# Row transposes by transposing transfers, two VectorE additions by accumulating transfers, and a new instruction order, in a four-layer graph-attention kernel

## Chip, cores and metric

The kernel runs on one core of a Trainium2 chip. The metric is the device time of one execution in microseconds. Three runs of the kernel before took 2677.28, 2681.27 and 2683.81 us, a median of 2681.27 us.

## What is computed

Eight graphs (batches) share one adjacency matrix of 2048 nodes; every node has 128 features. Four layers follow each other. Each normalises the rows of x, clips them at zero, attends over the neighbours and adds the result to x:

```python
h = jnp.maximum(_layernorm(x), 0.0)
# layers 0, 1, 3: scores are an outer sum
Wh = h @ W                       # layer 0: h @ W.T; layer 3: h = h*(node_weights+1) + node_bias before
                                 # W, and then a layer norm with ln_gamma, ln_beta on Wh
e = leaky_relu((Wh @ a1)[:, :, None] + (Wh @ a2)[:, None, :], 0.2)
p = softmax(where(adj > 0, e, -9e15))
out = p @ Wh                     # layer 0: elu(out); layer 1: out; layer 3: elu(out + Wh)
# layer 2: 4 heads of 32 features, scores from products
p = softmax(where(adj == 0, -inf, leaky_relu(h_head @ h_head.T, 0.2)))
out = p @ h_head
x = x + out
```

## The kernel before

**Units.** A unit is one layer of one batch, 32 in all: class Gat for layers 0, 1 and 3, class Heads for layer 2. A unit begins with row statistics (moments: BN_STATS on VectorE, a power on GpSimd). `rows_made` then makes the normalised rows h in four quarters of 512 rows on ScalarE (L538, for layer 3 also L545). `transposes` (L569) turns a quarter with four 128x128 TensorE transposes into PSUM, because the following products contract over features. In Gat, ScalarE copies the turned quarter to SBUF (`h_t`, L590), TensorE multiplies it with W and the two score vectors (L599), and ScalarE writes the weighted rows y and the exponential factors of the scores (L637 to L652). In Heads, the turned quarter is written as a coarse part `hi` (ScalarE, L964) and a rest `lo` (VectorE, L968); both go out to DRAM (L973), as do the rows themselves (`values`, L952), and come back by head as `s`, `m` and `v` (L987, L995, L1000).

**Tokens.** Gat's attention for half of the target nodes (1024) and one block of 128 source nodes is a token, 768 in all. VectorE makes the masked weights in one operation (`zg`, L767, named front), and TensorE multiplies them with y in eight products (L776, named back).

**Beats.** In Heads one head and one block of 128 source nodes is a beat, 512 in all: scores on TensorE in two pieces (L1063), two exponentials on ScalarE (L1070), one mask multiplication on VectorE (L1076), and sums by 32-column products on TensorE (`weigh`, L1085). These are issued for two beats at a time, for batch 7 for one.

**Ends.** `out` divides the sums of a half by their denominators (L808, L809). For layers 0 and 3 it then forms elu as two parts: an exponential (`oe`) and a clipped copy (`oa`), both at L815. VectorE adds min(exp, 1) to x (`elu_e`, L839), and the clipped part is added to x by an accumulating transfer that GpSimd issues (`plus_a`, L845). The -1 of elu is in x from the start: -2 is added to it once for both elu layers. Layer 3 also needs rows3's part (a transfer, L893), a multiplication by gamma (L832) and an addition of beta (L834) on VectorE. A head ends in `finish`: a division (L1105) and an accumulating transfer into x (L1110), issued by GpSimd.

**Order.** Nothing is scheduled by hand at the instructions. Every instruction group is registered with `add(engine, us, due, emit, needs, takes, frees, lag)`: an assumed duration, a due time, what it needs, which buffers it takes and frees, and a lag until its result is visible to others. `Plan.run` plays this list through and fixes the order on each of the five queues (TensorE, VectorE, ScalarE, GpSimd, and SP, which issues most transfers). All queues run in that order. Due times come from the tables TOKENS, BEATS and LEADS. Two PSUM slots named `pair` serve scores, transposes, projections and other short products.

Of the kernel before, what the change touches and what calls it, by code (L numbers as in the profile page):

```python
# [8 lines left out]
F32 = mybir.dt.float32  # L9
F32R = mybir.dt.float32r  # L10
BF16 = mybir.dt.bfloat16
I32 = mybir.dt.int32
U8 = mybir.dt.uint8
F8 = mybir.dt.float8e4
# [26 lines left out]
def adj_preln_d4(ctx: ExitStack, tc: tile.TileContext, x, adj, w0, a0, w1, a1, w3, a3,  # L41
# [112 lines left out]
    class Op:  # L154
# [6 lines left out]
    HURRY_US, WINDOW_US, BEAT_SUMS_US = 54.8, 0.148, 0.86  # L161

    EARLY = dict(front=30.31, score=69.21, exp=-934.15, mask=-178.47, sums=-6.09)

    SINGLY, GROUP = (7,), 2
# [3 lines left out]
    PLUS_US, PLUS_LAG_US, GATHER_US, GATHER_LAG_US = 1.0, 5.5, 2.2, 6.5  # L169


    SHIFTS = {
        30: 0.0, 93: 0.0, 113: 0.0, 115: 0.0, 121: 0.0, 131: 0.0, 135: 0.0, 139: 0.0, 143: 0.0, 147: 0.0,
        151: 0.0, 1041: 0.0, 1099: 0.0, 2060: 0.0, 2063: 0.0, 2886: 0.0, 2890: 0.0, 3168: 0.0, 3549: 0.0,
        5962: 0.0, 6178: 0.0, 6183: 0.0,
    }

    class Plan:
# [3 lines left out]
        LAG = dict(PE=0.3, ACT=0.22, DVE=0.15, POOL=0.2, SP=2.5)  # L182
        SAME = True
        ENTER_US, LEAVE_US = 0.09, 0.21
# [6 lines left out]
        def add(self, engine, us, due, emit, needs=(), takes=(), frees=(), lag=None, tiled=False):  # L191
            due += SHIFTS.get(len(self.ops), 0.0)
            op = Op(engine, us, due, emit, needs, takes, frees, self.LAG[engine] if lag is None else lag, tiled)
            self.ops.append(op)
            return op
# [56 lines left out]
    def fast(ctx):  # L252
# [9 lines left out]
        plan = Plan(dict(pair=(4, 6), sums=(0,), more=(1,), low=0, z=5, zg=3, r=2, h=3, h_t=2, hi=1, lo=1,  # L262
# [184 lines left out]
        class Unit:  # L447
# [15 lines left out]
            def moments(self, name, part, rows, needs):  # L463
# [21 lines left out]
                for q in range(4):  # L485
                    last = [add("DVE", 0.72, self.due(part + 0.03 * q), lambda op, q=q: stats(op, q),
                                last + list(needs[q]), takes=["st"] + ["norm"] * (name == "x") if q == 0 else [])]
                    if q == 0:
                        self.normal = taker = last[0]
                begun = add("DVE", 0.5, self.due(part + 0.11), begin, last, takes=["var"], frees=[("st", taker)])  # L490
                last = [add("POOL", 3.4, self.due(part + 0.12), power, [begun])]
# [37 lines left out]
            def rows_made(self, part, step):  # L529
# [4 lines left out]
                def rows(op, q):  # L534
                    self.h[q] = blocks(quarter("h", bufs=3))
# [27 lines left out]

            def transposes(self, q, part, made, takes):
# [6 lines left out]
                return add("PE", 0.45, self.due(part), turn, made[1:], takes=["pair"] + takes,  # L571
                           frees=[("h", made[0])])

        class Gat(Unit):
            def beginning(self):
# [6 lines left out]
                for q in range(4):  # L582
                    part = 0.2 + step * q
                    turn = self.transposes(q, part, made[q], ["h_t"])
# [3 lines left out]
                    def copy(op, q=q, turn=turn, begins=begins):  # L588
# [3 lines left out]
                    copied = add("DVE" if begins else "ACT", 0.61 if begins else 0.47, self.due(part), copy,  # L592
                                 [turn], frees=[("pair", turn)])
# [8 lines left out]
                    product = add("PE", 0.9, self.due(part + 0.03), project, [copied, projected[layer]],  # L602
# [10 lines left out]
                    ends.append(add("ACT", 0.55 if layer == 3 else 1.25, self.due(part + 0.05),  # L613
# [40 lines left out]
            def second(self, ends):  # L654
# [15 lines left out]
                scored = add("DVE", 0.7, self.due(0.8), scores, [last])  # L670
                powers = add("ACT", 0.3, self.due(0.81), exps, [scored])
                factored = add("DVE", 0.3, self.due(0.82), factors, [powers])
# [11 lines left out]
            def spread(self):  # L684
# [33 lines left out]
                if ROWS_TURNED:  # L718
# [14 lines left out]
                    turned = add("PE", 0.12, at, turn_rows, last, takes=["pair"])  # L733
                    last = add("ACT", 0.25, at, copy_rows, [turned], frees=[("pair", turned)])
                    self.written = add("SP", 0.5, at, write_rows, [last], lag=2.5)
# [4 lines left out]
            def targets(self, half, due):  # L740
# [9 lines left out]
                op = add("SP", 0.5, due, read, [self.written], takes=["r"], lag=6.5)  # L750
# [9 lines left out]
            def token(self, a, due, place, last_front, last_back, first, last, gate=None):  # L760
# [11 lines left out]
                def back(op):  # L772
                    z = self.z.pop(a)
                    for i in range(HB):
# [10 lines left out]
                b = add("PE", 1.785, due, back, [f, last_back, self.v_ready[jb // 4]],  # L785
                        takes=[name] + ["pair"] * place if first else [], frees=[("zg", f)])
# [9 lines left out]
            def out(self, half, back, place, name, due):  # L796
# [15 lines left out]
                def whole(op, into, func):  # L812
                    if into == "e" and "e" not in key:
                        key["e"] = big.tile([P, HB, C], F32, tag="oe", name="oe", bufs=1)
                    nc.scalar.activation(key[into], key["a"], func)  # L815

# [47 lines left out]
                else:  # L864
                    last = taker = add("DVE", 1.75, due - 30, divided, [back], takes=["oa"])
# [15 lines left out]
                if layer == 0:  # L881
                    e = e_taker = add("ACT", 0.95, due + 6, lambda op: whole(op, "e", AF.Exp), [last], takes=["oe"])
                    last = add("ACT", 0.95, due + 8, lambda op: whole(op, "a", AF.Relu), [e])
                else:
# [10 lines left out]
                    for k in range(L3_DMA and b != B - 1, 3):  # L895
                        last = add("DVE", 1.14, due + 6 + 4 * k, lambda op, k=k: wide3(op, k), [last] + rows)
                    e = add("ACT", 0.95, due + 18, lambda op: whole(op, "e", AF.Exp), [last])
# [24 lines left out]
                e = add("DVE", 1.14, late, elu_e, [e], frees=[("oe", e_taker)])  # L922
# [13 lines left out]
                last = add("SP", 0.5, late + 6, write, [last])  # L936
# [3 lines left out]
        class Heads(Unit):  # L940
            def beginning(self):
# [13 lines left out]
                for q in range(4):  # L955
                    part = 0.25 + step * q
                    kept = add("SP", 0.5, self.due(part), lambda op, q=q: keep(op, q), [kept, made[q][1]],
                               lag=2.5)
                    self.there.append(kept)
                    turn = self.transposes(q, part, made[q], ["hi", "lo"])  # L960

                    def high(op, q=q, turn=turn):
                        self.h_t[q, 0] = quarter("hi", F32R, 1)
                        nc.scalar.copy(self.h_t[q, 0], ps[:, turn.got["pair"], :])  # L964

                    def low(op, q=q, turn=turn):
                        self.h_t[q, 1] = quarter("lo", F32R, 1)
                        nc.vector.tensor_sub(self.h_t[q, 1], ps[:, turn.got["pair"], :],  # L968
                                             self.h_t[q, 0].bitcast(F32))
# [6 lines left out]
                    hi = add("ACT", 0.47, self.due(part), high, [turn])  # L976
                    lo = add("DVE", 0.61, self.due(part), low, [hi], frees=[("pair", turn)])
                    for k, (tag, op) in enumerate((("hi", hi), ("lo", lo))):
                        self.there.append(add("SP", 1.9, self.due(part + 0.02), lambda op, q=q, k=k: store(op, q, k),
                                              [op, kept], frees=[(tag, turn)], lag=2.5))  # L980

            def load(self, h, due):
# [29 lines left out]
                s0 = add("SP", 2.1, due, lambda op: source(op, 0), there, takes=["s"], lag=3.0)  # L1012
                m = add("SP", 1.0, due, target, there, takes=m_taken, lag=7.5)
                self.first_target = [m]
                m_taker = m if m_taken else held
                s1 = add("SP", 2.1, due + 4, lambda op: source(op, 1), self.there, takes=["s"], lag=3.0)
                v = add("SP", 0.5, due, values, self.there, takes=["v"], lag=5.5)
                return s0, s1, m, v, m_taker

            def beats(self, heads):  # L1020
# [4 lines left out]
                for h, (start, step) in enumerate(heads):  # L1025
                    ops = self.load(h, start - 24.0)
                    for jb in range(NB):
# [3 lines left out]
                        for c2 in range(2):  # L1031
                            score = add("PE", 0.463, due - EARLY["score"] + c2, lambda op, s=s, c2=c2: self.scores(op, s, c2),
                                        [score, ops[jb // HB], ops[2]], takes=["pair"] + ["z"] * (c2 == 0))
                            if c2 == 0:
                                z_taker = score
                            exps.append(add("ACT", 1.0, due - EARLY["exp"] + c2, lambda op, s=s, c2=c2, sc=score: self.exp(
# [380 lines left out]
```

## Time and profile before

| what | value |
|---|---|
| median of three runs | 2681.27 us |
| the profiled execution | 2679.22 us |
| its span, first to last instruction | 2677.4 us |
| granted TensorE clock, mean | 0.992 |

The largest groups of work, from the page's list of costliest groups:

| engine, line, what | count | busy us | mean ns |
|---|---|---|---|
| TensorE L776, products of tokens | 12288 | 1472.5 | 276 |
| TensorE L1063, scores of beats | 2048 | 627.0 | 421 |
| TensorE L1085, sums of beats | 4096 | 499.7 | 601 |
| TensorE L569, transposes of rows | 512 | 79.7 | 280 |
| VectorE L1076, masks of beats | 512 | 1160.0 | 2285 |
| VectorE L767, fronts of tokens | 768 | 969.4 | 1279 |
| ScalarE L538, rows | 512 | 207.0 | 485 |
| GpSimd L113, powers | 31 | 122.1 | 3940 |

Matmuls overlap in the pipeline, so a group's mean is the latency of one instruction; the pace is read from the starts of neighbouring groups in the timeline. A product of 4-byte values appears as two instructions. The waits say what a queue stood still for; the longest of TensorE's own (columns: us in total, times, longest) are 10.9 us for ScalarE's exponentials and 10.0 us for VectorE's fronts.

### The profile page before, as it was taken

Reading aid. Unit: us, or ns where it says so; the run is one execution under the profiler, and the core shown is the slowest. Engines: PE = TensorE matmul, PEld = TensorE weight load, DVE = VectorE, ACT = ScalarE, POOL = GpSimd, SP = SyncE. Lnnn points to the kernel's source line nnn. Section 1 sums busy time; section 2 is a strip of 40 time slices with the busy share of each in tenths; the row PEclk is TensorE's granted clock in tenths of the full one; section 3 lists DMA queues with packets and bytes.
Section 4 is the critical chain, followed back from the end, with each engine's and each line's share of the span. In section 5 each row is a group of like instructions: output and inputs, shape, how many; then the busy total and the mean of one; then the engine's idle time right before and its main releaser. Section 6 shows DMA issues by size and latency. Waiting matters only on the chain. (4 is left out here: it accounts for less than half of the span.)

```text
span 2677.4 us, 49161 instructions
## 1 busy us (share of the span) xinstructions
PE 2598.6 (97%) x20104; PEld 2041.9 (76%) x20104; DVE 2482.8 (93%) x3304; ACT 1719.8 (64%) x2777; POOL 279.8 (10%) x143
## 2 busy tenths in 40 slices
PE   7999999999999999999999999999999799999997
PEld 7899877687777786888777768787766478676587
DVE  8867989989999999999999999999999799999987
ACT  2526555767776677647766778674676866778751
POOL 1200000010100110011110101011101110010020
PEclk9999999999999999999999999999999999999999
DMA  9002423144344332362424434424315321542121
GB/s 319 17 9 63 97 52 67 10 94 103 81 88 99 62 62 56 60 123 56 86 50 87 79 78 87 82 48 88 72 42 93 64 40 56 115 68 64 33 52 34
DMA packets 216875, 196.49 MB, mean 73 GB/s; under 512 B 142896, under 2 KB 178176, under 8 KB 210496
## 3 DMA queue, kind: packets, MB, share of 16 engines
q1 hardware_dynamic: 144112, 156.46, 22.5%
q0 software_dynamic: 72112, 36.73, 12.0%
q8 instruction: 160, 2.62, 0.4%
q14 instruction: 75, 0.61, 0.1%
q10 hardware_dynamic: 416, 0.07, 0.0%
HBM read 123.03 MB, written 33.73 MB: 59 GB/s over the span
## 5 line engine op out<-in xcount | busy, mean ns | idle before, releaser
L776 PEld LDWEIGHTS ps<-y,zg 128*128 128x128 f32 x12288 | 1449.5, 192 | 66.1 <-DVE zg L767 17.0
L776 PE MATMUL ps<-y,zg 128*128 128x129 f32 x12288 | 1472.5, 276 | 13.6 <-DVE zg L767 10.0
L1070 ACT ACTIVATE z<-ps,shift 128x1024 f32<-128x1024 f32 x1024 | 1091.1, 1111 | 525.4 <-PE ps L1063 513.4
L1076 DVE SCALAR_TENSOR_TENSOR z<-z,edge 128x2048 f32<-128x2048 f32 x512 | 1160.0, 2285 | 26.9 <-ACT z L1070 26.6
L767 DVE SCALAR_TENSOR_TENSOR zg<-r,cr,edge 128x1024 f32<-128x1024 f32 x768 | 969.4, 1279 | 113.6 <-PE ps L776 101.9
L1063 PE MATMUL ps<-m,s 128*128 128x512 f32 x2048 | 627.0, 421 | 21.8 <-ACT z L1070 10.9
L1063 PEld LDWEIGHTS ps<-m,s 128*128 128x128 f32 x2048 | 341.0, 190 | 268.4 <-ACT z L1070 147.8
L1085 PE MATMUL ps<-z,v 128*32 128x512 f32 x4096 | 499.7, 601 | 1.5 <-DVE z L1076 1.3
L1085 PEld LDWEIGHTS ps<-z,v 128*32 128x32 f32 x4096 | 103.9, 109 | 223.8 <-issue 175.0
L538 ACT ACTIVATE h<-x,nmrx,rstdx 128x128 f32<-128x128 f32 x512 | 207.0, 485 | 48.5 <-DVE nmrx L118 36.0
L113 POOL TENSOR_TENSOR rstdx<-varx,neg_half 128x16 f32<-128x16 f32 x31 | 122.1, 3940 | 458.0 <-DVE varx L108 444.6
L1110 POOL DMA_DIRECT2D x<-o x31 | 65.8, 2124 | 747.9 <-DVE o L1105 608.2
L845 POOL DMA_DIRECT2D x<-oa x40 | 36.9, 922 | 748.5 <-ACT z L1070 199.5
L599 PE MATMUL ps<-rhs,h_t 128*128 128x130 f32 x768 | 104.9, 283 | 4.6 <-DVE h_t L590 2.7
L599 PEld LDWEIGHTS ps<-rhs,h_t 128*128 128x128 f32 x768 | 95.4, 195 | 12.6 <-ACT h_t L590 7.1
L471 DVE BATCH_NORM_STATS2 st<-x 128x6 f32<-128x128 f32 x496 | 100.4, 278 | 3.3 <-DMA x<-oa 3.3
L569 PE MATMUL ps<-ident,h 128*128 128x128 f32 x512 | 79.7, 280 | 4.2 <-ACT z L1070 1.7
L809 DVE TENSOR_TENSOR oa<-ps,rs 128x384 f32<-128x384 f32 x144 | 73.9, 513 | 5.1
L815 ACT ACTIVATE oe<-oa 128x1024 f32<-128x1024 f32 x32 | 33.9, 1058 | 69.0 <-DVE oa L834 55.3
L590 ACT COPY h_t<-ps 128x512 f32<-128x512 f32 x92 | 52.6, 585 | 33.2 <-PE ps L569 33.1
L569 PEld LDWEIGHTS ps<-ident,h 128*128 128x128 f32 x512 | 60.9, 143 | 16.6 <-ACT h L538 4.3
L637 ACT ACTIVATE y<-ps,y 128x128 f32<-128x128 f32 x240 | 68.6, 369 | 0.0
(129 smaller groups left out, 833.8 us busy)
## 6 DMA issues: line engine op xcount, KB each, us to landing
s<-halves SPq DMA_DIRECT2D x256, 128.0 KB, 2.8
m<-halves SPq DMA_DIRECT2D x64, 512.0 KB, 6.8
r<-row SPq DMA_DIRECT2D x42, 512.0 KB, 3.9
x<-oa POOLq DMA_DIRECT2D x40, 512.0 KB, 4.9
raw<-in_adj_dram SPq DMA_DIRECT2D x16, 1024.0 KB, 15.5
values<-h SPq DMA_DIRECT2D x32, 256.0 KB, 2.3
halves<-hi SPq DMA_DIRECT2D x128, 64.0 KB, 1.7
halves<-lo SPq DMA_DIRECT2D x128, 64.0 KB, 1.7
```

What stands on the lines that cost most here:

```text
L113: nc.gpsimd.tensor_tensor(out=rstd, in0=v, in1=neg_half, op=OP.pow)
L471: nc.vector.bn_stats(out=key["st"][:, n, :], in_=rows()[:, n, :])
L538: nc.scalar.activation(self.h[q][:, k, :], X[self.b][:, n, :], AF.Relu, scale=key["rstd"][:, n:n + 1], bias=key["nmr"][:, n:n + 1])
L569: nc.tensor.transpose(pk[:, k, :], self.h[q][:, k, :], ident)
L599: nc.tensor.matmul(pv[:, k, :C + 2], lhsT=self.h_t[q][:, k * P:(k + 1) * P], rhs=rhs, start=True, stop=True)
L767: nc.vector.scalar_tensor_tensor(z, self.r[half], self.cr[:, 0, jb:jb + 1], edge[:, jb, half * HN:(half + 1) * HN], op0=OP.max, op1=OP.mult)
L776: nc.tensor.matmul(ps[:, self.banks(half, place)[i // 3], k * CE:(k + 1) * CE], lhsT=z[:, i * P:(i + 1) * P], rhs=self.y[:, jb, :], start= ...
L809: nc.vector.tensor_mul(key["a"][:, i0:i1, :], pv[:, :, :C], r[:, i0:i1, None].to_broadcast([P, i1 - i0, C]))
L1063: nc.tensor.matmul(ps[:, lo + c, :], lhsT=self.S[h, jb // HB][:, at:at + P], rhs=self.M[h][:, (c2 * 2 + c) * 512:(c2 * 2 + c + 1) * 512], ...
L1070: nc.scalar.activation(self.z[s][:, c2 * HN:(c2 + 1) * HN], ps[:, lo:lo + 2, :].rearrange("p b t -> p (b t)"), AF.Exp, bias=shift)
L1076: nc.vector.scalar_tensor_tensor(self.z[s], self.z[s], 1.0, edge[:, jb, :], op0=OP.mult, op1=OP.mult, accum_out=self.den[:, h, jb:jb + 1])
L1085: nc.tensor.matmul(ps[c * HD:(c + 1) * HD, 0, :], lhsT=self.V[h][:, jb, :], rhs=z[:, c * 512:(c + 1) * 512], start=jb == 0, stop=jb == NB - 1,
```

## The change

1. The transposes of 25 of the 32 units leave TensorE; `ON_PE` lists the seven that stay. A quarter h is split on ScalarE into two planes of 16-bit halves (`pl`), one transposing transfer issued by SP turns both planes (`tr`), and ScalarE merges them to `h_t`. In Heads, `hi` and `lo` are then made from `h_t` in SBUF instead of PSUM; `lo` is written over `h_t`.
2. elu's exponential becomes exp(min(a, 0)), made by two ScalarE passes (`below`: clip of -a; `grown`: exponential of its negative) in place of one. Being at most 1, it needs no minimum, and an accumulating transfer issued by GpSimd adds it to x; batch 7 and the units in DIRECT keep VectorE.
3. Layer 3's addition of beta becomes an accumulating transfer too, except for batch 7.
4. The planner's assumed durations, lags and constants are other ones. TOKENS becomes a sequence of halves at equal steps (HALVES), in another order; BEATS becomes a list of 33 places between which a head's 16 beats are spread evenly; LEADS has other values. The empty SHIFTS go.
5. Buffers: h has two in place of three, `lo` goes, `pl` and `tr` have one each.

```diff
-    SINGLY, GROUP = (7,), 2
+    PLANES, TURNED, ON_PE = 1, 1, ((0, 0), (1, 0), (0, 1), (0, 2), (7, 1), (7, 2), (7, 3))
+    SPLIT_US, MOVE_US, MOVE_LAG_US, MERGE_US = 0.94, 1.28, 5.2, 1.207
+    GROUPS = (2, 2, 2, 2, 2, 2, 2, 2, 2, 2, 2, 2, 2, 2, 2, 2, 2, 2, 2, 2, 2, 2, 2, 2, 2, 2, 2, 2, 1, 1, 1, 1)
...
-        LAG = dict(PE=0.3, ACT=0.22, DVE=0.15, POOL=0.2, SP=2.5)
+        LAG = dict(PE=0.2, ACT=0.14, DVE=0.135, POOL=0.2, SP=1.6)
...
+            def turned_by_transfer(self, q, part, made, kept=None):
+                key = {}
+                def split(op):
+                    key["pl"] = big.tile([P, 2, 4 * P], U16, tag="pl", name="pl", bufs=PLANES)
+                    nc.scalar.copy(key["pl"], self.h[q].rearrange("p k c -> p (k c)").bitcast(U16).rearrange(
+                        "p (n two) -> p two n", two=2))
+                def move(op):
+                    key["tr"] = big.tile([P, 8, P], U16, tag="tr", name="tr", bufs=TURNED)
+                    nc.sync.dma_start_transpose(out=key["tr"], in_=key["pl"].rearrange("p two n -> p (two n)"))
+                def merge(op):
+                    self.h_t[q] = quarter("h_t")
+                    nc.scalar.copy(self.h_t[q].bitcast(U16).rearrange("p (n two) -> p two n", two=2),
+                                   key["tr"].rearrange("p (two k) n -> p two (k n)", two=2))
+                parted = add("ACT", SPLIT_US, self.due(part), split, made[1:], takes=["pl"], frees=[] if kept else [("h", made[0])])
+                moved = add("SP", MOVE_US, self.due(part), move, [parted, kept], takes=["tr"],
+                            frees=[("pl", parted)] + [("h", made[0])] * (kept is not None),
+                            lag=MOVE_LAG_US)
+                return add("ACT", MERGE_US, self.due(part), merge, [moved], takes=["h_t"], frees=[("tr", moved)])
...
+                def below(op):
+                    key["e"] = key.get("e") or big.tile([P, HB, C], F32, tag="oe", name="oe", bufs=1)
+                    nc.scalar.activation(key["e"], key["a"], AF.Relu, scale=-1.0)
+                def grown(op):
+                    nc.scalar.activation(key["e"], key["e"], AF.Exp, scale=-1.0)
...
-                    e = e_taker = add("ACT", 0.95, due + 6, lambda op: whole(op, "e", AF.Exp), [last], takes=["oe"])
+                    e_taker = add("ACT", 0.95, due + 6, below, [last], takes=["oe"])
+                    e = add("ACT", 0.95, due + 7, grown, [e_taker])
...
                     for k in range(L3_DMA and b != B - 1, 3):
+                        if k == 2 and b != B - 1:
+                            last = add("POOL", PLUS_US, due + 6 + 4 * k, lambda op: nc.gpsimd.dma_start(
+                                out=key["a"], in_=beta2_sb[:, None, :].to_broadcast([P, HB, C]), accum_op=OP.add),
+                                [last], lag=PLUS_LAG_US)
+                            continue
...
-                e = add("DVE", 1.14, late, elu_e, [e], frees=[("oe", e_taker)])
+                if (b, layer) in DIRECT or b == B - 1:
+                    e = add("DVE", 1.14, late, elu_e, [e], frees=[("oe", e_taker)])
+                else:
+                    e = add("POOL", PLUS_US, late, lambda op: nc.gpsimd.dma_start(
+                        out=xs(), in_=key["e"], accum_op=OP.add), [e], frees=[("oe", e_taker)], lag=PLUS_LAG_US)
...
-                    turn = self.transposes(q, part, made[q], ["hi", "lo"])
+                    by_pe = (self.b, 2) in ON_PE
+                    if by_pe:
+                        turn = self.transposes(q, part, made[q] + (kept,), [])
+                    else:
+                        turn = self.turned_by_transfer(q, part, made[q], kept)
...
-        TOKENS = {
-            (1, 0, 0): (92.0, 3.5), (0, 1, 0): (148.0, 3.5), (0, 1, 1): (204.0, 3.5), (1, 0, 1): (260.0, 3.5),
...
+        FIRST_HALF, PER_TOKEN = 92.0, 3.5
+        HALVES = (
+            (1, 0, 0), (1, 0, 1), (0, 1, 0), (0, 1, 1), (2, 0, 0), (2, 0, 1), (1, 1, 0), (1, 1, 1),
...
+        PLACES = (
+            137.932, 464.436, 478.603, 611.236, 636.894, 705.819, 824.15, 904.887, 899.992, 1059.234,
...
```

## The prediction

> **What bounds the kernel now.** I read the busy line first, then the stretches, then the waits of the engine that comes out busiest.
>
> ```profile
> PE 2598.6 (97%) x20104; PEld 2041.9 (76%) x20104; DVE 2482.8 (93%) x3304; ACT 1719.8 (64%) x2777; POOL 279.8 (10%) x143
> ```
>
> TensorE (PE) is out of work for 2677.4 - 2598.6 = 79 us, VectorE (DVE) for 195 us, ScalarE (ACT) for 958 us. The stretches (columns: us, then busy us of PE, PEld, DVE, ACT, POOL with their counts, the granted clock, the DMA share, GB/s) say where:
>
> ```profile
> 0.00:300.00 300.00, 275.38 (x2305) 260.44 (x2305) 230.72 (x400) 130.22 (x354) 36.35 (x27) 0.97 0.36 107
> 300.00:2000.00 1700.00, 1687.06 (x13041) 1310.61 (x13038) 1629.24 (x2094) 1139.73 (x1733) 176.07 (x84) 1.00 0.36 72
> 2000.00:2200.00 200.00, 181.68 (x1262) 120.84 (x1262) 178.26 (x230) 146.41 (x206) 21.81 (x9) 0.97 0.39 67
> 2200.00:2600.00 400.00, 394.08 (x2971) 290.18 (x2970) 384.50 (x520) 286.01 (x450) 43.82 (x22) 1.00 0.32 63
> ```
>
> From 300 to 2000 us PE idles 13 us in 1700. The rest of its idle time is the start (25 us), one poor stretch at 2000 to 2200 (18 us), 6 us after it, and the last 78 us (18 us, of which about 15 are the tail behind the last matmul, where VectorE divides and adds). DVE is only 4% behind PE in the long middle. So work taken off PE shortens the kernel only if about as much leaves DVE in the same stretches.
>
> **Part 1: 400 transposes leave PE.** The 32 units of (batch, layer) each turn four quarters of rows; seven stay on PE, so 25 x 4 = 100 quarters leave, four matmuls each. The instruction order agrees: 512 before, 112 after; all other PE matmuls have equal counts, and the 32-column products still stand in 281 runs (280 before), so no mode changes are saved. The group's 280 ns is latency with overlap, so I take the pace from PE's timeline:
>
> ```profile
> 551.90 0.60 PE L569 MATMUL ps<-ident,h 128*128 128x128 f32 x4
> 552.34 1.95 PE L776 MATMUL ps<-y,zg 128*128 128x129 f32 x16
> ```
>
> Four transposes hold PE for 552.34 - 551.90 = 0.44 us; ahead of a 32-column product 738.27 to 738.80, 0.53. 100 x 0.44 = **44 us** (53 at most). Each also held one of two PSUM pairs until ACT's copy ended; that relief I cost at nothing, with up to 5 us below.
>
> **Part 2: 40 wide operations leave DVE.**
>
> ```profile
> L839 DVE SCALAR_TENSOR_TENSOR x<-oe,x 128x1024 f32<-128x1024 f32 x32 | 39.1, 1221 | 2.0 <-ACT oe L815 2.0
> L834 DVE TENSOR_TENSOR oa<-oa,beta_sb 128x1024 f32<-128x1024 f32 x16 | 19.5, 1221 | 0.1
> ```
>
> 26 of the 32 and 14 of the 16 become accumulating transfers from POOL: 40 x 1.221 = 49 us off DVE, against 44 off PE. The gap between the two stays, so PE can take its whole gain. In their place POOL issues 40 transfers: the nearest row is x<-oa at 0.92 us and 4.9 us to landing; beta's, read in 512-byte pieces, lies between that and x<-o (128-byte pieces, 2.12 and 7.8 us), about 1.5 and 6. POOL goes from 280 to about 325 us: free. The next moments wait some 5 us longer per half; each unit's rows stand well ahead of their use, DVE waited for x<-oa 3.3 us in all, and I cost it at 0 to 5 us.
>
> **Part 3: ACT pays.** Its rows:
>
> ```profile
> L1070 ACT ACTIVATE z<-ps,shift 128x1024 f32<-128x1024 f32 x1024 | 1091.1, 1111 | 525.4 <-PE ps L1063 513.4
> L590 ACT COPY h_t<-ps 128x512 f32<-128x512 f32 x92 | 52.6, 585 | 33.2 <-PE ps L569 33.1
> L815 ACT ACTIVATE oe<-oa 128x1024 f32<-128x1024 f32 x32 | 33.9, 1058 | 69.0 <-DVE oa L834 55.3
> ```
>
> A quarter is split into two planes of 16-bit halves (1024 elements per partition) and merged again. The 1024-element SBUF row says 1.06 us for each: 100 x 2.12 = 212 us. No row has 2-byte elements at a stride: if they ran at half pace it would be 424 us, if faster 140; I take the row. 76 copies of 0.585 go (-44; layer 2's cast to hi stays). The new "below" pass adds 32 x 1.06 = 34. ACT becomes 1720 + 202 = 1922 us, 73% of about 2633. ACT waits 513 us for scores now, which is the cover. Without it (another 212 us: 81%, and crowded stretches over 90%) exponentials come late and PE stops.
>
> **Part 4: 100 transposing transfers on SP, and ACT waits for each.** Behind a merge in ACT's queue stand exponentials, for which the scores' PSUM pairs and the masks wait. So the landing time is the dear unknown.
>
> ```profile
> values<-h SPq DMA_DIRECT2D x32, 256.0 KB, 2.3
> v<-values SPq DMA_DIRECT2D x32, 256.0 KB, 3.8
> x<-o POOLq DMA_DIRECT2D x31, 256.0 KB, 7.8
> ```
>
> Plain transfers of the same 256 KB land in 2.3 to 3.8 us, 7.8 when cut into 128-byte pieces and issued by POOL. [...] I went through the changed order of ACT: between a split and its merge stand 1.3 to 18.5 us of its own work by the rows above, median about 6; at 73 to 80% load that passes in about 8 us. With 4 to 6 us, between v<-values and x<-o, which I take, the merge finds its data and the transfer costs nothing. [...]
> SP itself has room: one issue is 0.38 us for values<-h, 1.7 for a group of four; 100 x at most 1.7 = 170 us. What is moved behind them in SP's queue is the loads of s, m, v and r. SP waits for PE to free s (719 us now), so these loads are issued early, and PE waited for s only 5.5 us; I cost this at 0 to 10. The transfers add 26 MB and POOL's 21 MB to 196 MB, a DMA share of about 43% instead of 35%.
>
> **Part 5: the order.** The planner gets new durations, later landings and a new sequence of halves. From the built orders, per 100 us of PE work, I counted tokens (1.2 us of DVE each) and masks (2.29). In the late stretch at 2000 to 2400 DVE's share of these is 96, 91, 94 and 92 with some 14 of other work on top; before, the five from 1900 had 97, 92, 69, 99 and 91. So I don't credit the 18 us of the poor stretch: something like it stays. The first 300 us are as thin for DVE (165 against 169), and the tail for batch 7 keeps its DVE operations and PE transposes, plus one exp pass of 1.06 us. PE order effects: -15 to +25, taken at 0.
>
> **Sum.** PE 44 off, order 0, waits 0 net (pair relief against late transfers). The span 2677.4 becomes 2633; the profiled execution's 2679.2 becomes 2635. The median of the runs lies 2 us above that execution, well inside their spread of 6.5, so I give **2636 us**, 1.7% faster.
>
> **Rivals.**
> 1. *ACT becomes the bound through merges that wait* (slower). Place: the merge in ACT's queue, ahead of exponentials. [...] Strided 16-bit copies at half pace do it too: ACT at 81%, some 40 to 80 us on PE, 2675 to 2715. [...] Against it: 513 us of ACT waiting for PE, and the plain rows.
> 2. *DVE takes over as bound* in the stretches from 2000 to 2400: 93 + 14 per 100 us of PE work is 28 us too much over 400, against 18 lost before, and the same again in the heavy stretches around 300 and 700. Gain cut to 15 to 25 us: 2655 to 2665. For it: DVE at 96 to 99 in most stretches. Against it: it loses 49 us itself.
> 3. *Nothing much changes*: late loads of s and r, moments waiting for POOL's transfers, each a few us, give back 40: about 2678. For it: all queues are in order. Against it: compute engines waited some 42 us for transfers in the whole run, about 30 of it in the start.
> 4. *More than the sum*: PE idle of 2000 to 2200 also goes, the pairs relieve: 2635 - 18 - 7 = 2610.
>
> **Chances.** Forecast, 2620 to 2652: 0.45. Rival 4: 0.12. Rival 2: 0.15. Rival 3: 0.09. Rival 1: 0.19. A measurement of this kernel tells 0.3%, 8 us, from no change. Faster: 0.45 + 0.12 + 0.15 = 0.72; same 0.08; slower 0.20. The range runs from 2605 to 2700: it cuts off rival 1's upper two thirds and little below. Beside it, the likeliest case alone: 2620 to 2652.
>
> **What would show it.** Part 1: 112 matmuls of the identity with h, and PE busy near 2555. Part 2: DVE near 2435, 6 and 2 of the wide operations. Part 3: ACT near 1920; split and merge rows at 1.06 us. Part 4: the transposing transfer at 4 to 6 us to landing, and ACT's wait before the merge below 1 us on average; a wait of 2 us or more there, with PE's waits for ACT's z grown by tens of us, would make me wrong. Part 5: PE idle of 60 to 90 us in all; much more of it between 300 and 2400, ended by DVE's masks or fronts, would mean rival 2.

## The result and the profile after

The changed kernel takes **2647.55 us** (median of four runs, 2645.59 to 2654.17) against 2682.49 us for the kernel before on the same chip. The ratio is 0.9878 with a 95% interval of 0.9855 to 0.9900: 35 us faster. The forecast was 45 us faster, 2636 us. The execution that was profiled, 2654.17 us, is the slowest of the four, so its span of 2652.3 us shows some 7 us of loss that the median has not.

The busy line of the kernel after:

```profile
PE 2560.4 (97%) x19704; PEld 2006.4 (76%) x19704; DVE 2439.3 (92%) x3264; ACT 1914.6 (72%) x2933; POOL 316.8 (12%) x183
```

PE lost 2598.6 - 2560.4 = 38.2 us of work, but the profiled span shrank only by 25.1: PE's idle time grew from 78.8 to 2652.3 - 2560.4 = 91.9 us. The stretches of the kernel after (columns as in the prediction) say where. The last line is a part of the second:

```profile
0.00:300.00 300.00, 275.80 (x2351) 265.11 (x2352) 229.39 (x402) 134.91 (x355) 38.45 (x30) 0.98 0.35 104
300.00:2000.00 1700.00, 1668.43 (x12777) 1290.39 (x12776) 1609.43 (x2099) 1322.35 (x1922) 203.04 (x111) 0.99 0.51 96
2000.00:2200.00 200.00, 200.00 (x1488) 143.34 (x1490) 198.65 (x233) 146.13 (x187) 19.28 (x10) 1.00 0.43 82
2200.00:2600.00 400.00, 381.39 (x2796) 273.57 (x2789) 365.42 (x494) 302.69 (x458) 56.07 (x32) 0.98 0.47 78
...
1200.00:1300.00 100.00, 90.48 (x705) 73.86 (x706) 87.20 (x125) 72.20 (x121) 6.88 (x3) 0.95 0.39 66
```

The poor stretch at 2000 to 2200 is gone (18 us of PE idle before, none now). But 300 to 2000 went from 13 us of idle to 31.6, and 2200 to 2600 from 6 to 18.6. Ten of those 31.6 us lie in one place, from 1199 to 1209.5, and the granted clock of 1200 to 1300 is 0.95.

The waits of PE and of ACT in the kernel after (us in all, times, longest) name that place:

```profile
PE ps L800 <- DVE zg L791: 15.5, 14, 4.4
PE ps L1114 <- ACT z L1121: 11.6, 12, 3.5
PE ps L623 <- ACT h_t L575: 10.3, 1, 10.3
...
ACT h_t L575 <- DMA tr<-pl: 14.7, 5, 9.7
```

In sum PE waits longest for VectorE's fronts (15.5 us, 10.0 before) and for ScalarE's exponentials (11.6, 10.9 before), in many short waits. The longest single one is new: PE waited once, 10.3 us, for a merge (L575), and that merge waited 9.7 us for its transposing transfer. The timeline around it (start us, duration us, engine, operation, and in brackets the idle time before it and what ended it):

```profile
1188.14 1.92 PE L1136 MATMUL ps<-z,v 128*32 128x512 f32 x16
...
1189.04 2.13 POOL L1161 DMA_DIRECT2D x<-o  x1 [2.31 <-DVE rs L832]
...
1190.70 1.41 POOL L876 DMA_DIRECT2D x<-oa  x1
...
1191.34 21.07 SPq L571 DMA_TRANSPOSE tr<-pl  x2
...
1208.14 1.33 ACT L575 COPY h_t<-tr 128x1024 uint16<-128x1024 uint16 x1 [9.73 <-DMA tr<-pl]
...
1209.52 2.10 PE L623 MATMUL ps<-rhs,h_t 128*128 128x130 f32 x8 [10.26 <-ACT h_t L575]
1211.55 3.05 PE L1136 MATMUL ps<-z,v 128*32 128x512 f32 x16
```

At 1189 POOL issues a head's accumulating transfer (`x<-o`, 128-byte pieces), at 1190.7 half a unit's (`x<-oa`). At 1191.3 SP issues the transposing transfer of a quarter (its row joins the next one's issue); it lands 16.8 us later, where the median of the hundred is 3.2 us. ACT stands at the merge, the exponentials are behind it, and PE runs dry. The two accumulating transfers were late as well (last column: us from issue to landing, window 1180 to 1212); their medians are 5.3 and 8.0 us:

```profile
x<-oa POOLq DMA_DIRECT2D x1, 512.0 KB, 17.1
x<-o POOLq DMA_DIRECT2D x1, 256.0 KB, 16.5
```

After the stall sixteen 32-column products take 3.05 us, where sixteen took 1.92 us at 1188. The profile gives a granted clock of 0.50 for 1209.5 to 1213, and 1.00 again from 1214. The eight projections and these products take 2.2 us more than the same groups at 1222 (1.06 us for the projections) and 1188. So the stall of 10 us, with the slow stretch after it, costs an estimated 12, from these rows.

A second place is of the same kind. At 1915.8 SP issues two loads of `r`, between an `x<-oa` (1914.8) and a head's `x<-o` (1915.9). They land after 7.9 us, where 4.1 is the median of these loads. VectorE's front waits for them and PE for the front (window 1905 to 1930, us in all, times, longest):

```profile
DVE zg L791 <- DMA r<-row: 5.3, 1, 5.3
...
PE ps L800 <- DVE zg L791: 4.4, 1, 4.4
```

After this wait too the granted clock is low: 0.50 from 1924 to 1927, and 1.00 again from 1928. In all VectorE waited 17.7 us for `r` here, in five places, and before not once.

### The profile page after: what moved, and what is told of

It is laid out like the page before. It is cut to its first block, busy times and chain, and to the rows that moved or that the text cites. A ratio compares the mean times of both kernels' runs of the same rounds, so it can differ in the third digit from the quotient of the medians.

```text
span 2652.3 us, 48777 instructions
## 1 busy us (share of the span) xinstructions
PE 2560.4 (97%) x19704; PEld 2006.4 (76%) x19704; DVE 2439.3 (92%) x3264; ACT 1914.6 (72%) x2933; POOL 316.8 (12%) x183
## 5 line engine op out<-in xcount | busy, mean ns | idle before, releaser
L800 PEld LDWEIGHTS ps<-y,zg 128*128 128x128 f32 x12288 | 1453.3, 193 | 73.8 <-DVE zg L791 21.4
L800 PE MATMUL ps<-y,zg 128*128 128x129 f32 x12288 | 1471.3, 276 | 19.2 <-DVE zg L791 15.5
L1114 PE MATMUL ps<-m,s 128*128 128x512 f32 x2048 | 630.4, 422 | 15.9 <-ACT z L1121 11.6
L1114 PEld LDWEIGHTS ps<-m,s 128*128 128x128 f32 x2048 | 339.2, 190 | 257.3 <-ACT z L1121 134.1
L114 POOL TENSOR_TENSOR rstdx<-varx,neg_half 128x16 f32<-128x16 f32 x31 | 116.6, 3760 | 487.9 <-DVE varx L109 482.7
L575 ACT COPY h_t<-tr 128x1024 uint16<-128x1024 uint16 x100 | 135.5, 1355 | 19.1 <-DMA tr<-pl 14.7
L623 PE MATMUL ps<-rhs,h_t 128*128 128x130 f32 x768 | 106.9, 284 | 16.6 <-ACT h_t L575 10.3
L566 ACT COPY pl<-h 128x1024 uint16<-128x1024 uint16 x100 | 104.7, 1047 | 0.9
L843 ACT ACTIVATE oe<-oa 128x1024 f32<-128x1024 f32 x32 | 33.9, 1058 | 65.6 <-DVE oa L865 34.7
L963 POOL DMA_DIRECT2D x<-oe x26 | 25.2, 969 | 418.2 <-ACT oe L846 418.2
```

The costliest lines, as they stand in the source:

```text
L114: nc.gpsimd.tensor_tensor(out=rstd, in0=v, in1=neg_half, op=OP.pow)
L566: nc.scalar.copy(key["pl"], self.h[q].rearrange("p k c -> p (k c)").bitcast(U16).rearrange("p (n two) -> p two n", two=2))
L575: nc.scalar.copy(self.h_t[q].bitcast(U16).rearrange("p (n two) -> p two n", two=2), key["tr"].rearrange("p (two k) n -> p two (k n)", two=2))
L623: nc.tensor.matmul(pv[:, k, :C + 2], lhsT=self.h_t[q][:, k * P:(k + 1) * P], rhs=rhs, start=True, stop=True)
L800: nc.tensor.matmul(ps[:, self.banks(half, place)[i // 3], k * CE:(k + 1) * CE], lhsT=z[:, i * P:(i + 1) * P], rhs=self.y[:, jb, :], start= ...
L1114: nc.tensor.matmul(ps[:, lo + c, :], lhsT=self.S[h, jb // HB][:, at:at + P], rhs=self.M[h][:, (c2 * 2 + c) * 512:(c2 * 2 + c + 1) * 512], ...
```

## The experiments

All ratios are to the kernel before on the same chip, with 95% intervals.

### What a landing costs: two kernels of transfers alone

Both run a split, a transposing transfer and a merge eight times for each case. Their total time says nothing; the landings count. In the first, a POOL transfer is issued right ahead of the transposing one:

```diff
+    for n in range(ROUNDS):
+        o = small()
+        pl, tr = split("tr_gather")
+        nc.gpsimd.dma_start(out=xs[:, :, 0:32], in_=o, accum_op=OP.add)
+        nc.sync.dma_start_transpose(out=tr, in_=pl.rearrange("p two n -> p (two n)"))
+        merge(tr)
```

> Leaves out the whole computation: it only repeats split, transposing transfer and merge on one quarter of rows, eight times each alone, beside one accumulating transfer of 128-byte pieces, beside one of 4 KB pieces, beside one whose source is beta in 512-byte pieces, and beside the first two together. Theory (small pieces delay the transposing transfer): alone 3.0 to 3.3 us to landing, beside 4 KB pieces 4 to 5, beside beta's 5 to 7, beside 128-byte pieces 5 to 8, beside both 8 to 17. Rival (the late landings have another cause, such as loads from DRAM): 3 to 4.5 us in all of them.

The profile's issues of transfers in this kernel (last column: median us from issue to landing):

```profile
tr_alone<-pl SPq DMA_TRANSPOSE x8, 3.1
tr_gather<-pl SPq DMA_TRANSPOSE x8, 3.2
tr_plus<-pl SPq DMA_TRANSPOSE x8, 5.4
tr_beta<-pl SPq DMA_TRANSPOSE x8, 6.2
tr_both<-pl SPq DMA_TRANSPOSE x8, 7.1
```

Alone, eight blocks land in 3.1 us. Beside a 4 KB-piece `x<-oa` it is 5.4, beside beta's addition 6.2, beside a head's and `x<-oa` together 7.1. A head's transfer alone seemed harmless (3.2), against the suspicion from the timeline. Of the expected sizes beta's was met and the 4 KB pieces cost a little more; a head's alone and both together stayed below theirs at the median, though one of the eight landings beside both took 14.3 us. But the head's transfer and the transposing one were issued together here, and POOL is busy 2.1 us with the issue of a head's transfer: the transposing one may simply have been first. The second kernel shifts it:

```diff
+    def pause(k):
+        for _ in range(k):
+            nc.scalar.copy(pause_sb[:, :4 * P], hv)
+            nc.scalar.copy(pause_sb[:, 4 * P:], hv)
...
+    for k in range(4):
+        for n in range(ROUNDS):
+            o = small()
+            nc.gpsimd.dma_start(out=xs[:, :, 0:32], in_=o, accum_op=OP.add)
+            turned(f"tr_gather_{'abcd'[k]}", k)
```

> Leaves out the whole computation: it repeats split, transposing transfer and merge beside an accumulating transfer of 128-byte pieces, issued 0 to 3 steps of about 1 us ahead (a to d), and beside that one and one of 4 KB pieces issued after it (both, a to d), eight times each. Theory (the pieces delay a transposing transfer that starts while they are being moved): 3.1 us where the transfer gets ahead of them, 5 to 8 us where it starts in their midst, and over 10 us beside both for some steps. Rival: 3 to 4 us at every step beside the 128-byte pieces alone.

The same view of this kernel; a to d are 0 to 3 pauses of about 1.1 us:

```profile
tr_gather_a<-pl SPq DMA_TRANSPOSE x8, 3.2
tr_gather_b<-pl SPq DMA_TRANSPOSE x8, 6.3
tr_gather_c<-pl SPq DMA_TRANSPOSE x8, 5.6
tr_gather_d<-pl SPq DMA_TRANSPOSE x8, 4.3
...
tr_both_b<-pl SPq DMA_TRANSPOSE x8, 8.9
```

Issued 1.6 us after POOL began with the head's transfer, instead of 0.6 us (a), the landing doubles (6.3), and at the later steps, when less of that transfer's 7.0 us (median to landing here) is left, it falls to 5.6 and 4.3. With `x<-oa` behind it, it is 8.9 (10.3 at most; more than 10 had been expected for some steps). So a transposing transfer that starts amid a head's transfer lands later. Small pieces are not the only thing that does it: `x<-oa` with its 4 KB pieces costs 2.3 us too, and no case shifts that one alone. The 16.8 us of the kernel has the same neighbours, but is longer than any case here; how the rest of it comes about wasn't measured.

### Without the heads' transfers

After's order is kept, and only what one kind of operation emits is changed: each head's sum is added to x by VectorE at the place in the order where POOL's transfer stood.

```diff
-                    nc.gpsimd.dma_start(out=X[self.b][:, :, h * HD:(h + 1) * HD],
-                                        in_=key["o"].rearrange("p c k d -> p (c k) d"), accum_op=OP.add)
+                    gather_directly(op)
```

> The changed kernel in its own order, with the 31 heads' additions of 128-byte pieces made by VectorE at the place where the transfer stood (31 x 0.69 us, 21 us of VectorE). Theory (the late landings are made by the small pieces): no transposing transfer lands later than 7 us, the 10 us stall near 1200 us goes, half-clock stretches become fewer; against it stand VectorE's 21 us: 2635 to 2655 us. Rival (other transfers or ScalarE make the stalls): landings up to 10 us and more stay, and VectorE's part comes on top, 2655 to 2675 us.

Measured: **2635.35 us** (five runs, 2633.97 to 2638.33), ratio 0.9830 [0.9817, 0.9844]. Its interval lies clear of the changed kernel's, and it is the fastest kernel measured here. Its busy line, its long stretch, and the landings of its transposing transfers:

```profile
PE 2556.8 (97%) x19704; PEld 2003.7 (76%) x19704; DVE 2455.8 (93%) x3295; ACT 1914.9 (73%) x2933; POOL 250.3 (10%) x152
```

```profile
300.00:2000.00 1700.00, 1684.78 (x12928) 1298.62 (x12927) 1641.65 (x2141) 1340.80 (x1942) 155.27 (x89) 1.00 0.44 93
```

```profile
DMA to landing us min/median/max: 3.0/3.1/6.6
```

VectorE has 16.5 us more to do and still the kernel is 12 us faster. PE's idle time in 300 to 2000 fell from 31.6 to 15.2 us; in the whole it fell from 91.9 to 76.6. Both places above are gone: PE's wait for the merge is down from 10.3 us to 0.5, and from 1900 to 2000 PE is busy all the time (95.6 us in the changed kernel). They make 14.2 of the 16.4 us. (The two profiled executions differ by 19 us and the medians by 12, since the changed kernel's profile is of its slowest run.)

The longest landings of the transposing transfers over the runs point the same way: with the heads' transfers 16.8 us (changed kernel), 17.2 and 10.4 (next two sections), without them 6.6, and 7.7 and 7.1 in two more runs below. The next moments also have their x some microseconds earlier, and VectorE had waited 6.0 us for `x<-o`. At 1200 that wait ended at 1205.6, before the merge's data came at 1208.1, so there the late landing decided; for the rest this experiment doesn't part the two. Nor was the kernel before run without its heads' transfers, so it isn't shown how much it would gain.

### What TensorE's time is worth

Again after's order; 400 transposes of `h_t` are issued into the pair ahead of the projections of the units that no longer transpose on TensorE (layer 0 takes layer 2's share as well). Nothing reads them.

```diff
+                        for k in range(0 if (self.b, layer) in ON_PE else 8 if layer == 0 else 4):
+                            nc.tensor.transpose(ps[:, lo, k % 4 * P:(k % 4 + 1) * P],
+                                                self.h_t[q][:, k % 4 * P:(k % 4 + 1) * P], ident)
```

> The changed kernel in its own order, with 400 transposes put back on TensorE as idle work: ahead of a quarter's projection it turns h_t into the PSUM pair that the products then overwrite (4 or 8 a quarter, 44 us of TensorE at 0.44 us for four). Nothing else changes, neither order nor results. Theory (TensorE's time is the bound, microsecond for microsecond): 2685 to 2700 us. Rival (ScalarE or the transfers bound the changed kernel): 2650 to 2665 us.

Measured: 2687.37 us (eleven runs), ratio 1.0023 [1.0014, 1.0032], 40 us above the changed kernel. PE's busy time grew to 2595.7 us. The 400 transposes that were costed at 44 us bring 40 us back: TensorE is the bound, and nearly every microsecond taken from it counts. The late merge is there again in the same place: PE waits for it once, 10.7 us, and the longest landing is 17.2 us.

### What VectorE's time is worth

The same order, with the 26 additions of elu's exponential and the 14 of beta back on VectorE at the transfers' places:

```diff
-                    e = add("POOL", PLUS_US, late, lambda op: nc.gpsimd.dma_start(
-                        out=xs(), in_=key["e"], accum_op=OP.add), [e], frees=[("oe", e_taker)], lag=PLUS_LAG_US)
+                    e = add("POOL", PLUS_US, late, lambda op: nc.vector.tensor_add(
+                        xs(), xs(), key["e"]), [e], frees=[("oe", e_taker)], lag=PLUS_LAG_US)
```

(and the same for beta).

> The changed kernel in its own order, with the 26 additions of the exponential and the 14 of beta issued on VectorE at the place where the transfer stood (40 x 1.22 us, 49 us of VectorE); the order of the other queues is the changed kernel's. Theory (VectorE stands a few per cent behind TensorE, so its relief is what lets TensorE take its gain): 20 to 45 us slower than the changed kernel, 2668 to 2692 us. Rival (VectorE has 213 us of idle time and takes the 49 us for nothing): 2645 to 2655 us.

```profile
PE 2553.4 (97%) x19704; PEld 1998.2 (76%) x19704; DVE 2481.3 (94%) x3304; ACT 1913.8 (72%) x2933; POOL 271.1 (10%) x143
```

Its busy line shows VectorE 42 us busier, and the time is 2648.85 us, ratio 0.9884 [0.9869, 0.9900]: the same as the changed kernel within the intervals. The theory that the gain needs VectorE's relief missed; the rival held. There is a reservation: 40 transfers went as well (the longest landing is 10.4 us), so a loss on VectorE and a gain in landings may cancel. PE's waits show both: for fronts, masks and divisions of heads (19.2 us in the changed kernel) 30.1 us, for the merge 3.9 instead of 10.3, and for exponentials 7.0 instead of 15.3. Two more runs, without the heads' transfers, look at that. In the first, beta's additions go to VectorE too, in the second elu's as well, so that no addition by a transfer is left but `x<-oa`:

```diff
-                            last = add("POOL", PLUS_US, due + 6 + 4 * k, lambda op: nc.gpsimd.dma_start(
-                                out=key["a"], in_=beta2_sb[:, None, :].to_broadcast([P, HB, C]), accum_op=OP.add),
+                            last = add("POOL", PLUS_US, due + 6 + 4 * k, lambda op: nc.vector.tensor_add(
+                                key["a"], key["a"], beta2_sb[:, None, :].to_broadcast([P, HB, C])),
```

> The changed kernel in its own order, with the heads' 31 additions and beta's 14 on VectorE at the places of their transfers; the 26 additions of the exponential stay transfers. Theory (transfers of pieces of 512 bytes and less cause the long stalls, VectorE's time is free here): beta's late landings (13.7 us at most) go too, 2625 to 2636 us, faster than the changed kernel and than the one with the heads' additions alone moved. Rival (VectorE is full by now: 21 + 17 us on it): 2637 to 2650 us.

> The changed kernel in its own order, with the heads' additions, beta's and the exponential's all on VectorE (31 x 0.69 + 40 x 1.22 = 70 us): part 2 undone and the old 128-byte transfers gone as well. Theory: VectorE's busy time reaches about 2503 us, 95% of the span, and begins to cost: 2630 to 2650 us. Rival (VectorE still free): 2620 to 2632 us.

The busy line of the second, and three of PE's waits in it:

```profile
PE 2561.4 (97%) x19704; PEld 2003.4 (76%) x19704; DVE 2498.9 (94%) x3335; ACT 1913.9 (72%) x2933; POOL 205.7 (8%) x112
```

```profile
PE ps L800 <- DVE zg L791: 18.5, 20, 4.0
PE ps L1136 <- DVE z L1127: 12.7, 12, 2.3
...
PE ps L1114 <- DVE o L1156: 5.5, 4, 2.4
```

Measured: 2643.77 us (ratio 0.9850 [0.9835, 0.9865]; its five runs reach from 2634.80 to 2644.19) and 2652.64 us (0.9891 [0.9876, 0.9906]). Beta on VectorE should have gained up to 10 us and did not; its rival held. The second run lies just above its range. With all of them there the kernel is 17 us slower than with the heads alone, for 2498.9 - 2455.8 = 43 us more of VectorE. So VectorE's time does cost something once its slack is used: about 17/43 = 0.4 us for each, against 0.9 for TensorE. The longest landings were 7.7 and 7.1 us, near the 6.6 us of the run with the heads alone, so landings don't explain the difference. PE's waits do: for fronts, masks and divisions of heads they are 37.8 us here (the three lines and 1.1 us at another) and 21.0 us with the heads alone. That a kernel with VectorE at 94% loses nothing to one at 92% in the first of the three runs is then best read as two effects that cancel. The waits above support this; the two were not measured apart.

### What the order is worth

Three runs undo parts of the change through the planner, which then lays a new order. The first uses after's tables with the old operations (all transposes on TensorE, all additions on VectorE), the second also keeps the additions by transfers, the third does that with before's tables:

```diff
-    PLANES, TURNED, ON_PE = 1, 1, ((0, 0), (1, 0), (0, 1), (0, 2), (7, 1), (7, 2), (7, 3))
+    PLANES, TURNED, ON_PE = 1, 1, tuple((b, k) for b in range(8) for k in range(4))
```

> The changed kernel's planner, constants and sequence, with all 512 transposes back on TensorE and both additions (and the single exponential pass) back on VectorE and ScalarE: the order alone. Theory (the gain is the 44 us of TensorE work that left, and the order is worth nothing by itself): about the kernel before or a little slower, 2675 to 2710 us, since the places were searched for other operations. Rival (the better order makes the gain): 2640 to 2660 us.

> The changed kernel with the 400 transposes back on TensorE; the accumulating transfers stay. Theory (TensorE is the bound): TensorE busy rises by about 38 to 44 us and the time with it, 2680 to 2700 us. Rival (ScalarE's split, merge and waits have become a bound): the time stays within 10 us of 2648 or falls, since 100 x 1.8 us leave ScalarE.

> The kernel before's sequence and places, transposes on TensorE, with elu's and beta's parts added by transfers: part 2 alone. Theory (TensorE is the bound; VectorE's relief alone shortens little): 2665 to 2690 us, VectorE's busy time down by some 45 us. Rival (VectorE was the bound): 2640 us or less.

Measured: 2744.80 (1.0232 [1.0218, 1.0247]), 2764.89 (1.0310 [1.0296, 1.0324]) and 2752.70 us (1.0285 [1.0266, 1.0303]). All three missed by 35 to 65 us, on the slow side. A fourth run shows why they can't be read as prices of parts. It was meant as a test of the late landings. It changes no operation at all; a slot in the planner keeps transposing transfers and heads' transfers apart in time:

```diff
-                moved = add("SP", MOVE_US, self.due(part), move, [parted, kept], takes=["tr"],
+                moved = add("SP", MOVE_US, self.due(part), move, [parted, kept], takes=["tr", "quiet"],
...
-                    last = add("POOL", GATHER_US, due + 5, gather, [last], frees=[("o", turned)], lag=GATHER_LAG_US)
+                    last = add("POOL", GATHER_US, due + 5, gather, [last], takes=["quiet"], frees=[("o", turned)], lag=GATHER_LAG_US)
```

> The changed kernel, where the planner alone may not put a transposing transfer and a head's accumulating transfer of 128-byte pieces at the same time (one slot that both take; no wait is added on the chip). Theory (late landings of the transposing transfers, up to 16.8 us, come from the small-piece transfer beside them, and each such stall of TensorE also costs a stretch at half clock): the latest landing falls below 8 us, fewer half-clock stretches, 2630 to 2645 us. Rival (ScalarE's load, not the landings, costs the missing 11 us): no gain, 2645 to 2665 us.

Measured: 2721.67 us (1.0147 [1.0131, 1.0162]), 74 us above the changed kernel with the same operations and outside both ranges. The longest landing of a transposing transfer fell only to 9.4 us. Its long stretch:

```profile
300.00:2000.00 1700.00, 1641.21 (x12441) 1258.70 (x12440) 1572.80 (x2043) 1288.00 (x1867) 197.98 (x109) 0.98 0.49 93
```

PE idles 59 us here, against 31.6 in the changed kernel, and does 336 matmuls less in the same time. The due times fit one list of operations; any other list, or another rule between the same operations, gets an order that nobody chose. These four runs therefore tell nothing about a part.

The converse can be asked without a new order: what is the less work worth in before's order? This kernel keeps it and leaves out 300 of the 400 transposes (one block of a quarter stands for four) and the 40 additions of elu and beta.

```diff
-                    for k in range(4):
+                    for k in range(4 if (self.b, self.layer) in ((0, 0), (1, 0), (0, 1), (0, 2), (7, 1), (7, 2), (7, 3)) else 1):
```

> The kernel before in its own order, leaving out three of every four transposes of the 25 units (300, 33 us of TensorE; the turned quarter is one block repeated) and the 40 additions of the exponential and of beta (49 us of VectorE). No pass on ScalarE and no transfer is added. Theory (work taken off both engines shortens any order): 2645 to 2655 us. Rival (the order with its fixed waits holds the time, and the changed kernel's gain needed the new order): 2665 to 2680 us.

Its stretch at 2000 to 2200:

```profile
2000.00:2200.00 200.00, 183.22 (x1246) 123.36 (x1245) 175.70 (x236) 142.31 (x207) 24.90 (x9) 0.93 0.37 65
```

Measured: 2665.13 us, ratio 0.9938 [0.9924, 0.9952]: the theory missed, and the rival's range holds it just so. Some 33 us off TensorE (300 x 0.11) and 42 off VectorE's busy time became 16 us of time. TensorE's busy time fell by only 20.7 in the profiled execution, which is the slowest of the five and has a mean clock of 0.988 against 0.992 before. The poor stretch stands as it was, 17 us idle, at a clock of 0.93 where before had 0.97. In the new order 44 us off TensorE are worth 40; 33 in the old one are worth 16. So the old order gives back about half of what was costed. For all 400 that would be an estimated 22 us, where the changed kernel gained 35 with ScalarE's passes and the late landings on top: the new order is part of the gain. By itself it isn't seen to gain anything. The run with the 400 transposes given back has the new order and TensorE's old amount of work, with ScalarE's passes and the late landings, and takes 2687 us, 6 us more than before. The order seems to matter by letting the removed work count; how large its part is stays open, since no run has the new order with just the old operations.

## Why the prediction came out as it did

**What bounds the kernel** held: TensorE, at 97% before and after. That PE's gain needs as much off VectorE did not hold as stated: VectorE's 40 operations put back, without their transfers, cost 1 us, though the run with all additions on VectorE shows that its time isn't free (0.4 us per us).

**Part 1** (44 us off PE, busy near 2555): 38.2 us went, busy 2560.4. The run with the transposes given back puts 40 us on the same 400 in time. Part of the shortfall in busy time is the clock: at the mean of 0.988 the profiled span lost 0.012 x 2652 = 31.8 us of full speed, before 0.008 x 2677 = 21.4. Some of that lies in idle time, so the 10.4 us between them is an upper bound. "Relief of the pairs, up to 5 below" can't be seen.

**Part 2** (VectorE 2435, POOL 325; beta's transfer 1.5 us to issue and 6 to landing): 2439.3 and 316.8, with 1.6 and 7.0. The order of sizes by piece length, read from neighbouring rows, was right: 5.3 us to landing for `x<-oa`, 7.0 for beta's, 8.0 for `x<-o`. ACT waits 27.1 us in all for beta's transfers, which the sum left out. That this costs nothing isn't shown, but putting beta back on VectorE gained nothing.

**Part 3** (ScalarE 1920; split and merge 1.06 us each): 1914.6. The rows of the two copies in the kernel after:

```profile
L575 ACT COPY h_t<-tr 128x1024 uint16<-128x1024 uint16 x100 | 135.5, 1355 | 19.1 <-DMA tr<-pl 14.7
...
L566 ACT COPY pl<-h 128x1024 uint16<-128x1024 uint16 x100 | 104.7, 1047 | 0.9
```

The split reads 16-bit elements at a stride at the row's pace (1047 ns, the row 1058); the merge, which writes them at a stride, is 0.3 us dearer. Neither is the half pace that the first rival needed. That the total was met has luck in it. By the rows, split and merge take 104.7 + 135.5 = 240 us, 28 more than the 212 of the sum. But instructions of ACT overlap, so its rows add up to more than its busy time: they grew by 239 us, the busy line by 195.

**Part 4** (landing 4 to 6 us, the merge finds its data and the transfer costs nothing): this is **the step that failed in part**, and the mis-sized term of the sum. The typical landing was better than taken, 3.2 us. ACT's wait before merges averages 14.7/100 = 0.15 us, below the 1 us named. All eight 128 x 128 blocks of a quarter land in 3.1 us alone, like plain transfers of the same 256 KB in the kernel after (`values<-h` 2.4, `v<-values` 4.7). No run shows a landing time on which the first rival's upper times, beyond the range, could rest: the medians are 3.2 us in the kernel and 3.1 to 8.9 us in the two kernels of transfers alone. But the sum put one number on a thing with a tail. The tail is what the first rival described, ACT standing at a merge and PE behind it, at one place for 10 us instead of at a hundred. The loads behind them in SP's queue, costed at 0 to 10, have such a tail too: 4.4 us of PE at 1923. Taking away the heads' transfers took away both and gave 12 us: 2635.35. That this is the forecast's 2636 is chance, since VectorE does 16.5 us more there. So the term costed at zero was about 12, in which the earlier x for the moments has a part that wasn't measured apart. The DMA share was also higher than forecast, 47% instead of 43.

**Part 5** (order at 0, the poor stretch stays): the size was not far off, the place was wrong. The poor stretch vanished, and 18.6 + 12.7 us more of idle time came up in 300 to 2000 and 2200 to 2600, of which 15 are the two late landings. The total, 91.9 us, lies just above the 60 to 90 us forecast. Taking the order at 0 was too simple: in the old order less work gives about half of its costed worth.

**The rivals.** *ACT as the bound* happened once for 10 us, not throughout: PE's waits for exponentials at L1114 are 11.6 us, 10.9 before. *VectorE as the bound* was not the case where it was expected: from 2000 to 2200 it is at 99% and PE doesn't idle at all. It has a small part after that: from 2200 to 2600 PE waits 6.1 us for fronts, 3.3 before. *Nothing much changes* fell with the ratio. *More than the sum* held in its first half (the poor stretch went) and was eaten elsewhere.

## What to carry to other kernels

Price a new transfer by its slow landings (16.8 us here) and by what stands behind its waiter in an in-order queue, not by its median (3.2 us); keep long transfers in small pieces away in time from those that an engine will stand for (6.3 us to landing amid one, 3.1 alone), or give their work to an engine with slack. To learn what an engine's time is worth, give work back to it in an unchanged order: 0.9 us per us on TensorE here and between 0 and 0.4 on VectorE, though their busy shares were 97% and 92%. Where an order was searched for one list of operations, undoing a part through the planner measures another new order and not the part: change only what an operation emits.

## What the runs showed of the hardware

A transposing transfer of eight 2-byte 128 x 128 blocks lands 3.1 us after its issue begins; the issue holds its queue for 1.24 us. Issued 1.6 us after an accumulating transfer of 128-byte pieces it takes 6.3 us, with a 4 KB-piece transfer behind that 8.9, right behind a 4 KB-piece transfer alone 5.4, and 16.8 once in the kernel, where the accumulating transfers beside it took 16.5 and 17.1. An idle time of 10.3 us of TensorE was followed by a granted clock of 0.50 for about 4.4 us, one of 4.4 us by 0.50 for about 2.9. ScalarE's copy of 1024 16-bit elements per partition takes 1047 ns when it reads them at a stride and 1355 ns when it writes them so.
